# Message passing over 412500 edges: every gather with 125 rows, and one tile in eight groups fetched row by row by SyncE

## The chip, the cores and the metric

The kernel runs on one core of one Trainium2 chip. The metric is the device time of one execution in microseconds. Five engines work side by side, each in the order of its own instructions: TensorE (PE; its weight loads are listed as PEld), VectorE (DVE), ScalarE (ACT), GpSimd (POOL) and SyncE (SP), which here only issues DMAs. They wait for one another by semaphores.

## The reference

One layer of a graph network with 12500 nodes of 64 features and 412500 edges sorted by receiver. For every edge, the features of its sender, its receiver and the edge itself go through two small networks, one for a message and one for a logit; a softmax over all edges weighs the messages, and each receiver sums what it gets.

```python
h = jnp.maximum(_layernorm(x, axis=-1), 0.0)
msg_in = concatenate([h[src], h[dst], edge_attr_32], axis=-1)      # 412500 x 160
messages = swish(msg_in @ W1 + b1) @ W2 + b2
att = softmax(swish(msg_in @ Wa1 + ba1) @ Wa2 + ba2, axis=0)
aggregated = segment_sum(messages * att, dst, num_segments=12500)
out = x + swish(concatenate([h, aggregated], -1) @ Wu1 + bu1) @ Wu2 + bu2
```

## The kernel before

A prologue normalises the nodes and writes two tables to HBM: `ts_d` holds for each node its sender's part of both first layers (128 floats, 512 bytes), `tr_d` the receiver's part. The edges are then cut into 3304 tiles of `EP` = 125, and eight tiles (`K`) make a group `g`; there are 413 groups (`NG`). The loop over the groups is most of the time.

`load(g)` is written two groups ahead of `begin(g)` (`AHEAD`). It issues, on POOL, eight indirect DMAs (line 533) that gather the senders' rows of `ts_d` into `gs`, one of seven buffers of the pool `gather`. Tiles 0, 2, 4, 6 of a group gather 125 rows; tiles 1, 3, 5, 7 gather `WIDE` = 126, the last of which nobody reads. On SyncE it issues two loads of receiver rows into one of three `wins` buffers (line 554), whose address is a register read from `base_sb`, and for every fourth group the edge features (`eo`, line 544) and twice the receivers' numbers (`dbs`, line 547). VectorE turns those into a 0/1 matrix (line 558) and TensorE multiplies it with the window (line 562), which gives `pe`: receiver's part plus edge's part.

`begin(g)` adds the gathered rows to `pe` on VectorE (line 573) and takes the tanh on ScalarE (576). `end(g)` makes messages and logits on VectorE (586 to 597). Some groups later `by_node` builds weights (640) and TensorE sums the messages by receiver into `sp` (646); `out_of` copies `sp` on ScalarE (652), `project` multiplies it with the update's weights (657), and `put` adds the product to a table in SBUF (671, 675). A batch of four groups shares one running maximum of the logits.

All engines' orders are written out (`pin`). A buffer of `gs` is free again when `end` of its group has read it. The set `chosen`, whose tiles would be made from node features in SBUF instead of gathered, is empty in both kernels. Of the DMAs on the hardware queues, eight share eight semaphores in turn: each DMA waits for the one eight places before it, unless that is known to be done. The same holds for POOL's gathers among themselves.

Of the kernel before, what the change touches and what calls it, by code (L numbers as in the profile page):

```python
# [44 lines left out]
F32 = mybir.dt.float32  # L45
I32 = mybir.dt.int32
AF = mybir.ActivationFunctionType
ALU = mybir.AluOpType
AX = mybir.AxisListType
ENG = mybir.EngineType  # L50
# [3 lines left out]
P = 128  # L54
EP = 125
# [3 lines left out]
C = 2 * U  # L59
S1 = U + 1  # L60
K = 8
# [13 lines left out]
PHASE = 1  # L75
SLOTS = (((0, 24), (24, 24)), ((48, 24), (72, 12)), ((84, 24), (108, 17)))
ROUND = 12582912.0
WIDE = 126
EPS = 1e-5
NEG = -3.0e38  # L80
BIG = 3.0e38
# [5 lines left out]
WHY = "a receiver's number; windows past the last node are padded"  # L87
# [3 lines left out]
def gnn_kernel(ctx: ExitStack, tc: tile.TileContext, n_edges, x, src, src_row, dst, dst_row, first, edge,  # L91
# [73 lines left out]
    with tc.tile_pool(name="node1", bufs=1) as node1, \  # L165
# [134 lines left out]
        for c, nn in chunks:  # L300
            tr = node.tile([P, CB, C], F32, name="tr")[:, :nn, :]
            for b in range(0, nn, 4):
                n = min(4, nn - b)
                pn = node_ps.tile([P, 4, C], F32, name="pn", bufs=4)
                for i in range(0, n, 2):
# [7 lines left out]
        pin(nc.scalar.dma_start(hT_d, hT))  # L313

    one_pass(tc, n_edges, locals())
    again = nc.values_load(wrong[0:1, 0:1], min_val=0, max_val=1,
                           skip_runtime_bounds_check_because="it is the outcome of a comparison")
# [76 lines left out]
def one_pass(tc, n_edges, v):  # L394
    nc = tc.nc
    NB, T, NG, NP, NT = (v[k] for k in ("NB", "T", "NG", "NP", "NT"))
    ident, iota_w, bj, dloc, src_full, base_sb, real, unreal, far, wrong = (
        v[k] for k in ("ident", "iota_w", "bj", "dloc", "src_full", "base_sb", "real", "unreal",
                       "far", "wrong"))
    ts_d, tr_d, bq_d, xb_d, edge, dst_row = (  # L400
        v[k] for k in ("ts_d", "tr_d", "bq_d", "xb_d", "edge", "dst_row"))
    wa2, ba2_c, w2b, wu1a, wu2h, we, gather = (
        v[k] for k in ("wa2", "ba2_c", "w2b", "wu1a", "wu2h", "we", "gather"))
# [6 lines left out]
    pin = tc.keep_in_program_order  # L410

    with ExitStack() as ctx:
# [38 lines left out]
        for w in wins:  # L451
            nc.vector.memset(w, 0.0)
            for r in range(2):
                rows = slice(WR + r * DE, WR + (r + 1) * DE)
                nc.vector.tensor_copy(w[rows, :, r, :], we[rows, None, :].to_broadcast([DE, 2, C]))
        with tc.tile_pool(name="work2", bufs=2) as work2, \
                tc.tile_pool(name="small", bufs=3) as small, \
                tc.tile_pool(name="pre_ps", bufs=AHEAD + 1, space=PSUM) as pre_ps, \
                tc.tile_pool(name="one_ps", bufs=1, space=PSUM) as one_ps:
            pes, gss, lgs, ps_, psums, sps, pps, ees, mts, nums, cols = ({} for _ in range(11))  # L460


            w2t_ps = one_ps.tile([P, 4, P], F32, name="mt")[:U, 0, :S1]
# [8 lines left out]
            chosen = set()  # L472
# [23 lines left out]
            def columns(g, first, n):  # L496
                if g not in chosen:
                    return
                to, at = cols[g]
                _, regs = nc.values_load_multi_w_load_instructions(  # L500
                    at[0:1, first:first + n], engines=[ENG.Activation], min_val=0, max_val=NP // 2 - 1,
                    skip_runtime_bounds_check_because=WHY)
                for i in range(n):
                    pin(nc.scalar.copy(to[:, first + i:first + i + 1], hT[:, bass.ds(regs[i], 1)]))

            def burst(g, k):
                for i in range(EVERY):
                    columns(g + 3 + i, *SLOTS[EVERY - 1 - i][k])

            at_sp, at_lo, at_hi, bus, rest = {}, {}, {}, {}, {}  # L510


            tr_w = bass.AP(tensor=tr_d.tensor, offset=tr_d.offset,
                           ap=[[C, NP + WR - SHIFT], [SHIFT * C, 2], [1, C]])

            def registers(g, engine, at, base=base_sb, top=NP - 1):
                n = min(NQ, NG + (base is not base_sb) - g)
                _, regs = nc.values_load_multi_w_load_instructions(
                    base[0:1, g:g + n], engines=[engine], min_val=0, max_val=top,
                    skip_runtime_bounds_check_because=WHY)  # L520
                for i in range(n):
                    at[g + i] = regs[i]

            def load(g):

                t = g * K
                if g % NQ == 0:
                    registers(g, ENG.SP, at_sp)
                full = gather.tile([P, K, C], F32, name="gs")
                gs = gss[g] = full[:EP]  # L530
                for j in range(K - (g in chosen)):
                    rows = WIDE if j % 2 == 1 else EP
                    nc.gpsimd.indirect_dma_start(  # L533
                        out=full[:rows, j, :], out_offset=None, in_=ts_d[:, :],
                        in_offset=bass.IndirectOffsetOnAxis(ap=src_full[:rows, t + j:t + j + 1], axis=0))
                if g % NQ == 0:
                    n = min(NQ, NG - g) * E2
                    eo = eos[g // NQ % 2]
                    i = g // NQ % 2
                    db = dbs[i * WR:(i + 1) * WR].bitcast(I32)  # L540
                    for i in range(g, min(g + NQ, NG)):
                        e = slice((i - g) * E2, (i - g + 1) * E2)
                        ees[i] = eo[:, e], db[:, e]
                    nc.sync.dma_start(eo[WR:, :n],
                                      edge[:, g * E2:g * E2 + n])
                    for r in range(2):
                        nc.sync.dma_start(
                            db[r * R:(r + 1) * R, :n],
                            bass.AP(tensor=dst_row.tensor, offset=dst_row[r:r + 1, g * E2:].offset,
                                    ap=[[0, R], [1, n]]))  # L550
                eo, db = ees.pop(g)
                win = wins[g % WINS]
                for r in range(2):
                    nc.sync.dma_start(win[r * R:(r + 1) * R, :, r, :],
                                      tr_w[bass.ds(at_sp[g], R), :, :])
                for h in range(2):
                    e = slice(h * E2 // 2, (h + 1) * E2 // 2)
                    pin(nc.vector.tensor_scalar(eo[:WR, e], db[:, e], bj[g // NQ % 2 * WR:(g // NQ % 2 + 1) * WR, g, h:h + 1], None,  # L558
                                                op0=ALU.is_equal))
                pe = pes[g] = pre_ps.tile([P, K, C], F32, name="pe")[:EP]  # L560
                for q in range(H):
                    pin(nc.tensor.matmul(pe[:, 2 * q:2 * q + 2, :], eo[:, q * EP:(q + 1) * EP],  # L562
                                         win[:, q // 2, :, :], start=True,
                                         stop=q < H - 1 or g not in chosen))
                if g in chosen:
                    to, _ = cols[g]
                    pin(nc.vector.scalar_tensor_tensor(to, nums[g], half, to, op0=ALU.is_equal, op1=ALU.mult))
                    pin(nc.tensor.matmul(pe[:, K - 1, :], to, stack, start=False, stop=True))

            def begin(g):  # L570

                n = K - (g in chosen)
                pin(nc.vector.tensor_tensor(gss[g][:, :n, :], pes[g][:, :n, :], gss[g][:, :n, :], ALU.add))  # L573
                if n < K:
                    pin(nc.vector.tensor_copy(gss[g][:, n, :], pes[g][:, n, :]))
                pin(nc.scalar.activation(pes[g], gss[g], AF.Tanh))  # L576

            def end(g, then=None):
# [124 lines left out]
            at, weighed = [None, None], [0]  # L703
# [31 lines left out]
            for g in range(AHEAD):  # L735
                load(g)
            done = 0
            for g in range(NG):
# [4 lines left out]
                if more and g == NG - 1:  # L743
                    next(more)
                begin(g)
                if more and g < NG - 1:
                    next(more)
# [9 lines left out]
                if g + AHEAD < NG:  # L757
                    load(g + AHEAD)
# [36 lines left out]
                if g >= 16 and g // 8 - 2 < NT:  # L795
# [3 lines left out]
                    elif g % 8 in (0, 3, 6):  # L799
# [3 lines left out]
                                         engines=[ENG.SP, ENG.DVE, ENG.PE, ENG.Activation])  # L803


            two, one = at[1], at[0]
# [334 lines left out]
```

## Time and profile before

| | before |
|---|---|
| time, three runs | 5157.05, 5168.84, 5172.98 us; median 5168.84 |
| the profiled execution | 5172.98 us; span 5171.3 us, 1.7 us outside it |
| mean granted TensorE clock | 0.595 of full |
| busy: PE, DVE, ACT, POOL | 2470.4, 3165.5, 608.2, 3674.5 us |
| gathers (line 533) | 3304, first at 51.2 us, last at 5068.8 us |
| window loads (line 554) | 826 |
| gather queue, hardware DMA queue | 17.8% and 13.1% of 16 engines' span |

The busy time of an engine counts the instructions themselves. Behind the bar in a group's row stand its busy time and the mean of one in ns, behind the second bar the time that the engine stood idle just before such an instruction, with what ended most of it. "issue" means that the profile shows nothing that the engine waited for, "remote" that a semaphore update ended the wait whose sender the view doesn't name. Beginning and end of the loop take 152.5 us together.

### The profile page before, as it was taken

How to read it: one execution, taken by the hardware profiler on the slowest of the kernel's cores; microseconds unless marked ns; L12 is line 12 of the kernel's file. 1: busy time of each engine (PE TensorE's matmuls, PEld its weight loads, DVE VectorE, ACT ScalarE, POOL GpSimd, SP SyncE). 2: the span in 40 equal slices, each digit the busy share in tenths (PEclk: the TensorE clock that was granted, in tenths of full speed). 3: DMA queues.
4: the chain of work that ended last, by engine and by line, in shares of the span. 5: the costliest groups of instructions: out<-in, count | busy, mean ns of one | idle time of the engine just before them, and what ended most of it. 6: DMA issues, size and time to landing. Idle time of an engine off the chain costs nothing. (4 is left out here: it accounts for less than half of the span.)

```text
span 5171.3 us, 46541 instructions
## 1 busy us (share of the span) xinstructions
PE 2470.4 (48%) x11247; PEld 1946.3 (38%) x11247; DVE 3165.5 (61%) x8745; ACT 608.2 (12%) x1250; POOL 3674.5 (71%) x3329
## 2 busy tenths in 40 slices
PE   5254544544454544444544544444444444444545
PEld 4243433433343433333333433333333333333435
DVE  6366666666665656565655656665656555655757
ACT  3011111111110111111110111111111111110112
POOL 4777677677677677777777777777777777777772
PEclk8555565665555556665655556665656555655656
DMA  7233333333333323323323322322323323323322
GB/s 242 64 80 74 78 88 74 79 80 78 75 74 70 71 64 73 73 67 72 73 66 70 73 67 69 74 67 70 72 65 73 73 64 73 73 65 72 73 66 69
DMA packets 315703, 393.24 MB, mean 76 GB/s; under 512 B 153249, under 2 KB 244478, under 8 KB 315042
## 3 DMA queue, kind: packets, MB, share of 16 engines
q0 software_dynamic: 211456, 214.45, 17.8%
q1 hardware_dynamic: 102594, 166.10, 13.1%
q10 hardware_dynamic: 1376, 9.67, 0.5%
q8 instruction: 92, 1.51, 0.1%
q14 instruction: 185, 1.52, 0.1%
HBM read 362.26 MB, written 25.72 MB: 75 GB/s over the span
## 5 line engine op out<-in xcount | busy, mean ns | idle before, releaser
L533 POOL DMA_INDIRECT gs<-ts_d,src_sb x3304 | 3657.3, 1107 | 1410.1 <-issue 1377.3
L562 PE MATMUL pe<-wins,eo 128*125 128x256 f32 x3304 | 1497.2, 631 | 1055.7 <-issue 453.6
L562 PEld LDWEIGHTS pe<-wins,eo 128*125 128x125 f32 x3304 | 1000.4, 317 | 1348.9 <-issue 518.5
L657 PE MATMUL mt<-ss,w2u 65*128 65x40 f32 x826 | 224.4, 369 | 1336.6 <-issue 703.3
L657 PEld LDWEIGHTS mt<-ss,w2u 65*128 65x128 f32 x826 | 209.4, 293 | 1536.3 <-issue 970.7
L640 DVE TENSOR_SCALAR wt<-iota_w,dloc,p 125x40 f32<-125x40 f32 x3304 | 760.1, 342 | 5.0
L646 PE MATMUL sp<-wt,acts 125*65 125x40 f32 x6608 | 714.6, 286 | 3.6 <-DVE wt L640 2.7
L646 PEld LDWEIGHTS sp<-wt,acts 125*65 125x65 f32 x6608 | 678.9, 205 | 7.7 <-DVE wt L640 3.4
L675 DVE TENSOR_TENSOR sums<-sums,mt 64x40 f32 x606 | 116.0, 191 | 854.1 <-remote 734.0
L576 ACT ACTIVATE pe<-gs 125x1024 f32<-125x1024 f32 x413 | 424.7, 1028 | 1600.3 <-DVE gs L573 759.1
L573 DVE TENSOR_TENSOR gs<-pe,gs 125x1024 f32<-125x1024 f32 x413 | 503.1, 1218 | 50.3 <-issue 30.7
L671 DVE SCALAR_TENSOR_TENSOR sums<-sums,scale,mt 64x40 f32 x220 | 56.1, 255 | 594.5 <-remote 446.3
L652 ACT COPY ss<-sp 65x40 f32<-65x40 f32 x413 | 77.4, 187 | 2543.9 <-remote 2380.3
L592 DVE SCALAR_TENSOR_TENSOR pe<-pe,gs 125x512 f32<-125x512 f32 x413 | 288.9, 699 | 14.0
L594 DVE TENSOR_TENSOR pe<-pe,w_all 125x512 f32<-125x512 f32 x413 | 288.7, 699 | 13.8
L586 DVE SCALAR_TENSOR_TENSOR acts<-pe,gs 125x512 f32<-125x512 f32 x413 | 285.6, 692 | 15.7 <-issue 3.1
L597 DVE TENSOR_REDUCE lg<-pe 125x8 f32<-125x512 f32 x413 | 284.0, 688 | 11.0
L558 DVE TENSOR_SCALAR eo<-dbs,bj 64x250 f32<-64x250 int32 x826 | 274.4, 372 | 16.1 <-DMA dbs<-in_dst_row_dram 7.8
L678 DVE COPY stand<-nmax 64x40 f32 x826 | 181.8, 220 | 2.0 <-issue 1.4
L616 PE MATMUL mt<-ident,mx 125*128 125x125 f32 x110 | 46.4, 421 | 269.7 <-remote 124.5
L623 DVE TENSOR_REDUCE gm<-mt 128x1 f32<-128x125 f32 x110 | 31.1, 282 | 200.7 <-remote 200.1
L357 DVE TENSOR_SCALAR bu<-mt,w_all 64x256 f32<-64x256 f32 (+1 forms) x50 | 23.9, 478 | 170.0 <-remote 124.6
(113 smaller groups left out, 571.3 us busy)
## 6 DMA issues: line engine op xcount, KB each, us to landing
gs<-ts_d,src_sb POOLq DMA_INDIRECT x3304
eo<-in_edge_dram SPq DMA_DIRECT2D x103, 500.0 KB
dbs<-in_dst_row_dram SPq DMA_DIRECT2D x206, 250.0 KB
wins<-tr_d SPq DMA_DIRECT2D x826, 32.0 KB
ts_d<-ts SPq DMA_DIRECT2D x5, 896.0 KB
tr_d<-tr ACTq DMA_DIRECT2D x5, 896.0 KB
hT_d<-hT ACTq DMA_DIRECT2D x1, 3136.0 KB
xt<-in_x_dram SPq DMA_DIRECT2D x24, 128.0 KB
```

The source lines that it names most:

```text
L533: nc.gpsimd.indirect_dma_start(out=full[:rows, j, :], out_offset=None, in_=ts_d[:, :], in_offset=bass.IndirectOffsetOnAxis(ap=src_full[:ro ...
L558: pin(nc.vector.tensor_scalar(eo[:WR, e], db[:, e], bj[g // NQ % 2 * WR:(g // NQ % 2 + 1) * WR, g, h:h + 1], None, op0=ALU.is_equal))
L562: pin(nc.tensor.matmul(pe[:, 2 * q:2 * q + 2, :], eo[:, q * EP:(q + 1) * EP], win[:, q // 2, :, :], start=True, stop=q < H - 1 or g not in ...
L573: pin(nc.vector.tensor_tensor(gss[g][:, :n, :], pes[g][:, :n, :], gss[g][:, :n, :], ALU.add))
L576: pin(nc.scalar.activation(pes[g], gss[g], AF.Tanh))
L586: pin(nc.vector.scalar_tensor_tensor(acts[g % ACTS][:, :, 0:U], th[:, :, U:C], 1.0, gs[:, :, U:C], op0=ALU.add, op1=ALU.mult))
L592: pin(nc.vector.scalar_tensor_tensor(att, th[:, :, 0:U], 1.0, gs[:, :, 0:U], op0=ALU.add, op1=ALU.mult))
L594: pin(nc.vector.tensor_tensor(att, att, wa2[:EP, None, :].to_broadcast([EP, K, U]), ALU.mult))
L597: pin(nc.vector.tensor_reduce(lgs[s][:, k:k + K], att, AX.X, ALU.add))
L640: pin(nc.vector.tensor_scalar(wt[:, j, :], iota_w[:EP, j // H, :], dloc[:, g * K + j:g * K + j + 1], p[:, k + j:k + j + 1], op0=ALU.is_equ ...
L646: pin(nc.tensor.matmul(sp, acts[g % ACTS][:, j, :], wt[:, j, :], start=j == 0, stop=j == K - 1))
L657: pin(nc.tensor.matmul(pp, w2u.rearrange("s h u -> s (h u)"), sps.pop(g), start=True, stop=True))
```

## The change

All gathers have 125 rows. In groups 8, 16, ..., 408 (51 of them) the last tile is not gathered by POOL: SyncE fetches its 125 rows one at a time into a buffer of its own, `alone[g]`. The eight groups before it share that work: in each `load`, behind the window loads, SyncE reads up to 16 row numbers into registers (line 540) and issues as many DMAs of one row, 512 bytes (line 546). The row numbers of a tile come by one small DMA some groups earlier. `begin(g)` of such a group adds seven tiles at once and the eighth by an addition of its own.

```diff
-WIDE = 126
+QUEUES = [(ENG.SP, 8, 0, 16)]
...
+            def single(q, g):
+                if g < NG - 4:
+                    t = g * K + K - 1 - (g in chosen)
+                    rows_at[q, g] = small.tile([1, EP], I32, name=f"one_src{q}", bufs=2)
+                    nc.sync.dma_start(rows_at[q, g], v["src_row"][:, t * EP:(t + 1) * EP])
+
+            def rows(q, g):
+                engine, every, phase, n_rows = QUEUES[q]
+                if g == 0:
+                    single(q, phase + every)
+                if g < phase:
+                    return
+                at = (g - phase) % every
+                g = g - at + every
+                if at == 0:
+                    rows_at.pop((q, g - every), None)
+                    if (q, g) in rows_at:
+                        alone[g] = work2.tile([EP, C], F32, name=f"one_gs{q}")
+                if at == every // 2:
+                    single(q, g + every)
+                if (q, g) not in rows_at:
+                    return
+                a = at * n_rows
+                n = min(n_rows, EP - a)
+                if n <= 0:
+                    return
+                loads, regs = nc.values_load_multi_w_load_instructions(
+                    rows_at[q, g][0:1, a:a + n], engines=[engine], min_val=0, max_val=NP - 1,
+                    skip_runtime_bounds_check_because=WHY)
+                for one in loads:
+                    pin(one)
+                for k in range(n):
+                    pin(dma[engine].dma_start(alone[g][a + k:a + k + 1, :], ts_d[bass.ds(regs[k], 1), :]))
...
-                full = gather.tile([P, K, C], F32, name="gs")
-                gs = gss[g] = full[:EP]
-                for j in range(K - (g in chosen)):
-                    rows = WIDE if j % 2 == 1 else EP
+                gs = gss[g] = gather.tile([P, K, C], F32, name="gs")[:EP]
+                for j in range(K - (g in chosen) - (g in alone)):
                     nc.gpsimd.indirect_dma_start(
-                        out=full[:rows, j, :], out_offset=None, in_=ts_d[:, :],
-                        in_offset=bass.IndirectOffsetOnAxis(ap=src_full[:rows, t + j:t + j + 1], axis=0))
+                        out=gs[:, j, :], out_offset=None, in_=ts_d[:, :],
+                        in_offset=bass.IndirectOffsetOnAxis(ap=src_sb[:, t + j:t + j + 1], axis=0))
...
                 for r in range(2):
                     nc.sync.dma_start(win[r * R:(r + 1) * R, :, r, :],
                                       tr_w[bass.ds(at_sp[g], R), :, :])
+                for q in range(len(QUEUES)):
+                    if QUEUES[q][0] == ENG.SP:
+                        rows(q, g)
...
             def begin(g):
-                n = K - (g in chosen)
+                n = K - (g in chosen) - (g in alone)
                 pin(nc.vector.tensor_tensor(gss[g][:, :n, :], pes[g][:, :n, :], gss[g][:, :n, :], ALU.add))
+                if g in alone:
+                    pin(nc.vector.tensor_tensor(gss[g][:, n, :], pes[g][:, n, :], alone.pop(g), ALU.add))
```

More of the change, by code (lines that the diff above doesn't have):

```diff
@@ L396, in one_pass @@
     NB, T, NG, NP, NT = (v[k] for k in ("NB", "T", "NG", "NP", "NT"))
-    ident, iota_w, bj, dloc, src_full, base_sb, real, unreal, far, wrong = (
-        v[k] for k in ("ident", "iota_w", "bj", "dloc", "src_full", "base_sb", "real", "unreal",
+    ident, iota_w, bj, dloc, src_sb, base_sb, real, unreal, far, wrong = (
+        v[k] for k in ("ident", "iota_w", "bj", "dloc", "src_sb", "base_sb", "real", "unreal",
                        "far", "wrong"))
@@ L459, in one_pass @@
                 tc.tile_pool(name="one_ps", bufs=1, space=PSUM) as one_ps:
-            pes, gss, lgs, ps_, psums, sps, pps, ees, mts, nums, cols = ({} for _ in range(11))
+            pes, gss, lgs, ps_, psums, sps, pps, ees, mts, nums, cols, alone = ({} for _ in range(12))
             w2t_ps = one_ps.tile([P, 4, P], F32, name="mt")[:U, 0, :S1]
@@ L508, in burst @@
                     columns(g + 3 + i, *SLOTS[EVERY - 1 - i][k])
+            rows_at = {}
+            dma = {ENG.SP: nc.sync, ENG.Activation: nc.scalar}
+            def single(q, g):
[30 more added lines that the diff above has]
+                    pin(dma[engine].dma_start(alone[g][a + k:a + k + 1, :], ts_d[bass.ds(regs[k], 1), :]))
             at_sp, at_lo, at_hi, bus, rest = {}, {}, {}, {}, {}
@@ L570, in begin @@
             def begin(g):
-                n = K - (g in chosen)
+                n = K - (g in chosen) - (g in alone)
                 pin(nc.vector.tensor_tensor(gss[g][:, :n, :], pes[g][:, :n, :], gss[g][:, :n, :], ALU.add))
-                if n < K:
-                    pin(nc.vector.tensor_copy(gss[g][:, n, :], pes[g][:, n, :]))
+                if g in alone:
+                    pin(nc.vector.tensor_tensor(gss[g][:, n, :], pes[g][:, n, :], alone.pop(g), ALU.add))
+                if g in chosen:
+                    pin(nc.vector.tensor_copy(gss[g][:, K - 1, :], pes[g][:, K - 1, :]))
                 pin(nc.scalar.activation(pes[g], gss[g], AF.Tanh))
```

## The prediction

> **What bounds the kernel now.** I read the page's table of engines first, then its costliest groups, then the waits, then the timeline of one cycle.
>
> ```profile
> span 5171.3 us, 46541 instructions
> ...
> PE 2470.4 (48%) x11247; PEld 1946.3 (38%) x11247; DVE 3165.5 (61%) x8745; ACT 608.2 (12%) x1250; POOL 3674.5 (71%) x3329
> ...
> L533 POOL DMA_INDIRECT gs<-ts_d,src_sb x3304 | 3657.3, 1107 | 1410.1 <-issue 1377.3
> ```
>
> POOL does one thing, the 3304 gathers, and looks 71% busy. Its idle time says more: 1410 us are mostly the 0.30 us that follow each gather (3303 x 0.30 = 1000 us). Another 49 us lie before the first gather, and 359 us remain (85 gaps in the trace): there POOL stands before a group's first gather because none of the seven `gs` buffers is free. So neither side is the bound alone. POOL would need 11.3 us a group, the loop takes 12.15 us (5018.8 us from first gather to last, over 413 groups), and POOL is held up now and then by the consumers.
>
> ```profile
> ACT ss L652 <- remote: 2380.3, 246, 27.0
> POOL gs L533 <- issue: 1377.3, 3246, 48.8
> ```
>
> The consumers are held up too, by something that this view can't name ("remote"). The timeline shows it at the end of one cycle (start, us, then the instruction and the idle time before it):
>
> ```profile
> 2616.24 1.21 DVE L573 TENSOR_TENSOR gs<-pe,gs 125x1024 f32<-125x1024 f32 x1
> ...
> 2622.42 1.96 PE L646 MATMUL sp<-wt,acts 125*65 125x40 f32 x16
> ...
> 2640.25 1.21 POOL L533 DMA_INDIRECT gs<-ts_d,src_sb  x1 [0.30 <-issue]
> 2641.76 1.00 POOL L533 DMA_INDIRECT gs<-ts_d,src_sb  x1 [0.30 <-issue]
> 2644.58 0.19 ACT L652 COPY ss<-sp 65x40 f32<-65x40 f32 x1 [21.48 <-remote]
> ...
> 2646.28 1.21 DVE L573 TENSOR_TENSOR gs<-pe,gs 125x1024 f32<-125x1024 f32 x1
> ...
> 2652.57 1.21 POOL L533 DMA_INDIRECT gs<-ts_d,src_sb  x1 [9.81 <-issue]
> 2653.81 1.23 DVE L573 TENSOR_TENSOR gs<-pe,gs 125x1024 f32<-125x1024 f32 x1 [0.19 <-issue]
> ```
>
> The matmuls into `sp` were put through at 2622.4. ScalarE's copy of `sp` starts 22 us later, two microseconds after POOL has stopped. Between, the semaphore updates recorded for TensorE come about one per gather: of 3155 gaps between them in the run, 734 are 1.3 to 1.6 us. When POOL stops, the rest arrives at once. The group that began (L573) at 2616.24 therefore waits 30 us for its successor, while the next takes 7.5 us. One cycle of eight groups, between the stalls that end at 2552.61 and 2652.57, has four groups of 7.2 to 7.8 us and four of 17.4 us on average: 100 us, of which POOL's 64 gathers are 90 and a stall 9.8.
>
> **First part: 125 rows for 126.** The timeline gives the price of one row. The durations alternate, and the even tile of a pair is the 125-row one:
>
> ```profile
> 2637.43 1.21 POOL L533 DMA_INDIRECT gs<-ts_d,src_sb  x1 [0.30 <-issue]
> 2638.94 1.00 POOL L533 DMA_INDIRECT gs<-ts_d,src_sb  x1 [0.30 <-issue]
> ```
>
> Start to start, in the 3218 spacings without a stall, a 125-row gather takes 1.518 us and a 126-row gather 1.304: the wider one is 0.214 us cheaper. Each group loses four cheap ones; of the 1652, 51 disappear in the second part, so 1601 x 0.214 = **+342 us** of POOL time.
>
> The Trainium skill, page "DMA: Bandwidth & Descriptors", section "Why a DMA increments its semaphore by 16 and not by 1", says that a DMA is spread over the largest number of engines up to 16 that divides its rows: 5 for 125, 14 for 126. The packets of this trace agree: 47908 of 4096 B and 31388 of 512 B on the gather queue, 14.5 and 9.5 a gather, the means of 5 x (3 + 1) and 14 x (1 + 1) packets. The page prices no gather; were the price one per data packet, 125 rows (20 packets) would be cheaper than 126 (28), this term would be at most nothing, and the sum would end at 5106.
>
> **Second part: one tile in eight groups leaves POOL.** Groups 8, 16, ..., 408 gather seven tiles. That is 51 gathers fewer, always the eighth, a 126-row one: 51 x 1.304 = **-67 us**. POOL then needs 3253 x 1.518 / 413 = 11.96 us a group.
>
> **What SyncE takes over.** Each of those tiles costs 125 one-row DMAs, each with its register instruction, 16 a group behind the group's two window loads, one load of 16 registers a group, and one load of row numbers per eight groups. The nearest row is the second window load, which is also addressed by a register:
>
> ```profile
> L554 SPq MOVE wins<-tr_d x826: 3/29/1345, 81.3 to 5078.4; - x166
> L554 SPq DMA_DIRECT2D wins<-tr_d x826: 4/317/1685, 81.3 to 5078.5; - x166
> ```
>
> From the start of the first to the start of the second it is 0.52 us where POOL is idle (57 pairs), 0.74 on average while POOL gathers (356 pairs), median of all 0.65. A DMA of a single row in the prologue (`base_sb`) took 0.31 us to issue, like the 0.32 here, so a smaller transfer will not be cheaper. SyncE's group holds 15.6 rows, two windows, 0.9 of the other loads (rounded into 18.5 DMAs) and some 0.3 us of register loads: 9.9 us at 0.52, 12.3 at 0.65, 14.0 at 0.74. The loop after the change takes (5018.8 + 275) / 413 = 12.8 us a group. It is covered by SyncE's idle time (it mostly waits for TensorE to free a window) as long as a DMA costs under (12.8 - 0.3) / 18.5 = 0.68 us. I take 0.65, the median, and so nothing on the path; if the cover is gone, see the first rival. Every row DMA also waits for the DMA eight before it. A window's last packet starts 1.2 us after issue, and eight issues take 4 us, so that wait is met, except behind the edge load (4.2 us, once in four groups). Behind a waiting row stand the next group's window loads, for which TensorE waits; three window buffers give them about two groups of slack.
>
> The page named above also says, under "Rules for kernel authors", to coalesce small transfers, and gives a fixed cost of some 2.0 us per DMA. Taken one after another, that would be an estimated 250 us a tile, or 31 us a group, and a time above 12000. The trace issues the next DMA after 0.5 to 0.7 us.
>
> **VectorE** gets 51 extra additions of 125x128 (0.2 to 0.35 us by its small rows) and the first addition shrinks by an eighth of 1.22 us in the same groups: within 10 us either way, covered by its 39% idle time.
>
> **POOL's stalls.** The sum turns on the 359 us. Both ends: all gone (-359), if the consumers stay at 12.15 us a group; grown, if SyncE joins them. I keep them, because in the slow half of a cycle the consumers are clocked by the gathers: about one TensorE update per gather. A gather that takes 1.518 instead of 1.411 us makes the four slow groups 7.6% longer: 69.6 x 0.076 = 5.3 us per 100, or 5019 x 0.053 = +266 us. That is the same as the POOL sum, 342 - 67 = +275, reached from the other side.
>
> **Sum:** own time of the profiled run 5173.0 (span 5171.3 and 1.7 outside), plus 275 = **5448 us**. The median shown is 5168.8, 4 us lower, within the spread of the runs.
>
> **The rivals.** *SyncE becomes the bound (slower still).* It decides from 0.68 us a DMA. For it: the mean with POOL busy is 0.74, and its slow cases look clocked by the gathers as well. Against: the median is under the limit, and a loop that lags gives POOL pauses in which a DMA costs 0.52. At 0.74 a group fits 16.2 DMAs into POOL's 11.96 us and the other 2.3 at 0.52 into a pause: 13.5 us with the register loads, 413 x 13.46 + 152.5 outside the loop + 1.7 = 5713. *The stalls are eaten up (faster).* If the slow half is not clocked by gathers but by a fixed time, the consumers keep 12.15 us, POOL's 11.96 fills their time, and both terms pass without stalls: 5173 + 275 - 359 = 5089. It turns faster from the point where over 275 of the 359 us are absorbed. For it: POOL's own need stays below the consumers' present pace. Against: the recorded updates keep step with the gathers. *The width is not what makes the odd gather cheap.* If it is the place in a pair, the mean of 1.411 stays, and 51 x 1.411 = -72 us gives 5101. Against: nothing else differs between the two, and the packets do.
>
> **How the numbers follow.** Stalls kept: 0.50, 5448. Half of them absorbed: 0.05, 5270. SyncE the bound: 0.26, 5570 to 5720. Absorbed: 0.14, 5089. Width without effect: 0.05, 5101. A measurement of this kernel can tell about 0.3%, 15 us, from no change; a landing there needs stalls absorbed almost exactly, 0.03 taken from the two faster cases. So faster 0.16, same 0.03, slower 0.81. The range goes from 5140 to 5720: it leaves out the two faster cases and a little above the dearest SyncE.
>
> **What would show it.** Right: all gathers 1.21 us and none of 1.00, 3253 of them, POOL near 3960 us busy, stalls of about 360 us still there, L652's wait not shorter. Wrong: mean gather under 1.15 us; stalls gone; or POOL's stalls above 500 us with TensorE waiting for `wins`, which would be SyncE.

## The result and the profile after

The changed kernel takes 5052.34 us (5051.23 to 5052.72, four runs), the kernel before in the same comparison 5167.32 us (5157.05 to 5172.98): a ratio of 0.978, 95% interval 0.976 to 0.980. The forecast was 5448 us, slower.

One thing must be known to read these numbers. The kernel before takes about 5160 us in the recorded pair and on chip 13, and 4762 to 4771 us on chips 0, 3, 4, 14 and 15. The one profile of it from there (chip 3) has under 4 us of pauses in which POOL stands before a full set of buffers. Against that faster before, the changed kernel is 5.8% slower (below).

The page of after, its engines and the groups that answer to those of before:

```profile
span 5050.3 us, 66258 instructions
...
PE 2353.8 (47%) x11247; PEld 1896.7 (38%) x11247; DVE 3219.3 (64%) x8796; ACT 589.2 (12%) x1250; POOL 3964.8 (79%) x3278
...
L569 POOL DMA_INDIRECT gs<-ts_d,src_sb x3253 | 3947.6, 1214 | 1044.1 <-issue 947.7
```

The gathers (now line 569) are as forecast: 3253 of them, POOL 3965 us busy, 1.21 us each. But idle before them is 1044 us, and 3252 gaps of 0.305 us are 992 of it. The first wait for the table is another 48. Only 4 us are left of the 359 that POOL stood before a group. The waits and the timeline say the same (start, us, instruction, and in brackets the idle time before it):

```profile
DVE gs L612 <- DMA gs<-ts_d,src_sb: 1449.4, 350, 7.5
POOL gs L569 <- issue: 947.7, 3104, 0.3
```

```profile
2614.85 1.21 POOL L569 DMA_INDIRECT gs<-ts_d,src_sb  x1 [0.30 <-issue]
2616.37 1.21 POOL L569 DMA_INDIRECT gs<-ts_d,src_sb  x1 [0.30 <-issue]
2617.03 1.22 DVE L612 TENSOR_TENSOR gs<-pe,gs 125x1024 f32<-125x1024 f32 x1 [3.50 <-DMA gs<-ts_d,src_sb]
2617.89 1.21 POOL L569 DMA_INDIRECT gs<-ts_d,src_sb  x1 [0.31 <-issue]
2619.26 0.18 ACT L693 COPY ss<-sp 65x40 f32<-65x40 f32 x1
```

The direction of waiting has turned. VectorE waits for gathers in 350 of the 413 groups, the longest pause between two gathers is 2.4 us where it was 12.6, and the copy of `sp`, which had waited 2380 us for "remote" updates, starts without a bracket. (The 48.8 us in before's "issue" row is the wait for the table ahead of the first gather; after's row books that wait under the table's DMA.) POOL's gathers alone set the time. In the spans: gathers without their pauses +276 us (3253 x 1.518 for 1652 x 1.518 + 1652 x 1.304), pauses 359 to 4, -355, and the stretch behind the last gather's start 102 to 57 us, because the consumers no longer trail the gathers (the addition to `pe` began 52 to 67 us behind its group's last gather in most groups, now 2 to 7), -45. The sum is -124, measured 5050.3 - 5171.3 = -121.

### The profile page after: what moved, and what is told of

Its sections match the earlier page's. It is cut to its first block, busy times and chain, and to the rows that moved or that the text cites. A ratio compares the mean times of both kernels' runs of the same rounds, so it can differ in the third digit from the quotient of the medians.

```text
span 5050.3 us, 66258 instructions
## 1 busy us (share of the span) xinstructions
PE 2353.8 (47%) x11247; PEld 1896.7 (38%) x11247; DVE 3219.3 (64%) x8796; ACT 589.2 (12%) x1250; POOL 3964.8 (79%) x3278
## 5 line engine op out<-in xcount | busy, mean ns | idle before, releaser
L569 POOL DMA_INDIRECT gs<-ts_d,src_sb x3253 | 3947.6, 1214 | 1044.1 <-issue 947.7
L601 PE MATMUL pe<-wins,eo 128*125 128x256 f32 x3304 | 1527.3, 641 | 1746.5 <-DVE eo L597 1091.6
L601 PEld LDWEIGHTS pe<-wins,eo 128*125 128x125 f32 x3304 | 1022.2, 325 | 2049.0 <-DVE eo L597 1188.3
L612 DVE TENSOR_TENSOR gs<-pe,gs 125x1024 f32<-125x1024 f32 (+1 forms) x413 | 498.7, 1208 | 1463.1 <-DMA gs<-ts_d,src_sb 1449.4
L687 PE MATMUL sp<-wt,acts 125*65 125x40 f32 x6608 | 628.7, 266 | 8.8 <-DVE wt L681 4.9
L687 PEld LDWEIGHTS sp<-wt,acts 125*65 125x65 f32 x6608 | 591.2, 181 | 16.3 <-DVE wt L681 7.1
L597 DVE TENSOR_SCALAR eo<-dbs,bj 64x250 f32<-64x250 int32 x826 | 296.1, 398 | 85.2 <-DMA dbs<-in_dst_row_dram 77.7
L698 PE MATMUL mt<-ss,w2u 65*128 65x40 f32 x826 | 186.0, 319 | 197.9 <-DVE gm L664 160.7
L719 DVE COPY stand<-nmax 64x40 f32 x826 | 212.7, 257 | 0.8 <-issue 0.2
L668 ACT ACTIVATE scale<-fall 128x1 f32<-128x1 f32 x110 | 22.4, 204 | 581.2 <-DVE nmax L665 274.0
```

Source lines behind the costliest of these rows:

```text
L569: nc.gpsimd.indirect_dma_start(out=gs[:, j, :], out_offset=None, in_=ts_d[:, :], in_offset=bass.IndirectOffsetOnAxis(ap=src_sb[:, t + j:t ...
L687: pin(nc.tensor.matmul(sp, acts[g % ACTS][:, j, :], wt[:, j, :], start=j == 0, stop=j == K - 1))
L698: pin(nc.tensor.matmul(pp, w2u.rearrange("s h u -> s (h u)"), sps.pop(g), start=True, stop=True))
```

## The experiments

Two questions: do the two gather terms hold, and what removed the pauses? All kernels are the changed one with the width of each of a group's eight gathers, `WIDTHS`, and the list `QUEUES` set as said; with `QUEUES` empty SyncE fetches no rows and POOL gathers 3304 tiles. `before` and `after` were also run unchanged. Where an expected text names a theory by a letter, what is compared here is the time that it gives. "Hold-up" is the lateness of TensorE's semaphore updates that the forecast saw in before's trace. In e5 the seven buffers are also named one by one and cleared at the start, because ten of their rows are never gathered.

**Each part alone, and other widths** (chip 4, before 4763.28 us).

```diff
-QUEUES = [(ENG.SP, 8, 0, 16)]
+QUEUES = []
+WIDTHS = (125,) * 8               # e1
+WIDTHS = (126,) * 8               # e3
+WIDTHS = (115,) * 8               # e5: ten rows of each tile are not gathered
+                                  # e2: QUEUES kept, WIDTHS = (125, 126) * 4
```

> The first part alone: every tile gathered with 125 rows, no tile by SyncE. Theory A (the 14-engine gathers of 126 rows are what holds up TensorE's semaphore updates): the hold-up is gone as in the changed kernel, POOL is busy without a pause, and the 51 gathers that come back cost 51 x 1.518 = 77 us more than the changed kernel: 5050 + 77 = 5129 us; ScalarE's wait before the copy of sp stays near 60 us in all. Theory B (SyncE's row DMAs are what removed the hold-up): the waits before the copy of sp come back with over 1500 us, POOL pauses for 300 us or more, 5450 to 5520 us. Theory C (POOL's faster pace caused it: 11.3 us a group against 11.96): at 12.14 us a group it is gone too, 5129 us.

Measured 5115.84 us, ratio 1.074 (1.072 to 1.076). Over before +352.6 us; 1652 x 0.214 is 353.5.

> The second part alone: one tile in eight groups by SyncE, and the odd tiles still gather 126 rows. Theory A: the hold-up stays (over 1500 us of waiting before the copy of sp, POOL pauses of 300 us or more), and the time stays within some 100 us of the kernel before: 5070 to 5250 us. Theory B: no hold-up, POOL's own pace is the time: 1652 x 1.518 + 1601 x 1.304 + 110 outside = 4705 us. Theory C: POOL is even quicker than before (11.13 us a group), so the hold-up stays, 5070 to 5250 us.

Measured 4695.9 us, ratio 0.986 (0.984 to 0.987): -67.4 us, and 51 x 1.304 is 66.5.

> Every tile gathered with 126 rows, no tile by SyncE: twice as many wide gathers as before. POOL alone would need 3304 x 1.304 + 110 = 4418 us. Theory A: the hold-up is at least as long as before, 5150 us or more, and the gain in POOL's pace turns into pauses of POOL (600 us or more). Theory C: the same sign, as POOL is faster still. If both are wrong and the hold-up comes from the alternation of the two widths, it is gone and the time is 4420 to 4600 us.

Measured 4409.39 us, ratio 0.926 (0.924 to 0.927).

> Every tile gathers only its first 115 rows (115 is divided by 5 and by nothing more up to 16, like 125); the last ten rows of each tile are left at zero or stale, so ten edges of each tile are computed without their sender. A gather should take about 1.0 to 1.15 us and 0.30 us behind it, so that POOL's pace is about the 1.41 us of the kernel before, without wide gathers. Theory A (number of engines): no hold-up, POOL busy without a pause, 3304 x 1.36 to 1.43 + 110 = 4600 to 4850 us. Theory C (pace): at the pace of before the hold-up returns, over 1500 us of waiting before the copy of sp, and 5100 us or more.

Measured 5025.59 us, ratio 1.055 (1.053 to 1.057). The gather rows of e3 and e5:

```profile
L572 POOL DMA_INDIRECT gs<-ts_d,src_sb x3304 | 3291.6, 996 | 1056.4 <-issue 963.6
```

```profile
L581 POOL DMA_INDIRECT gs<-ts_d,src_sb x3304 | 3905.5, 1182 | 1061.0 <-issue 899.3
```

126 rows cost 0.996 us and 115 rows 1.182: fewer rows, dearer gather. In all four the idle time before gathers is, to 3 us, only their 0.30 us each and the first wait, and the times follow POOL's sum. Both terms of the forecast hold, each to 1 us. The expectations of 5150 or more for e3 fall: wide gathers do not make POOL pause on this chip, and neither does the mix of before, which ran beside them at 4763.

**The pair again, and 128 and 127 rows** (chip 3, before 4761.94 us over 13 runs).

```diff
+WIDTHS = (128,) * 8               # f1, QUEUES kept
+WIDTHS = (127,) * 8               # f3, QUEUES = []
```

> The kernel before, unchanged, for a profile beside the one shown. Theory D (the hold-up of TensorE's updates is a state that the alternating gathers can be in or not, independent of the kernel's text): either the profile shows the hold-up and 5157 to 5173 us again, or none of it and POOL's own pace as the time: 1652 x 1.518 + 1652 x 1.304 + 110 = 4772 us. Theory E (the hold-up always comes with this kernel): ScalarE's wait before the copy of sp near 2400 us and over 5100 us whatever the chip.

Measured 4762.46 us, ratio 1.000 (0.999 to 1.001). Its waits beside the recorded ones of before show what is missing:

```profile
DVE gs L573 <- DMA gs<-ts_d,src_sb: 1288.9, 369, 8.7
...
POOL gs L533 <- issue: 947.4, 2953, 47.8
```

Same instructions, same gathers (1.104 us on average, recorded 1.107), but no "remote" wait at all, and VectorE waits for gathers. Of TensorE's recorded updates, 32 gaps are 1.3 to 1.6 us, where the recorded profile has 734. So the kernel alone does not bring the hold-up.

> The changed kernel, unchanged, on the same chip as the repeated kernel before. If POOL's gathers alone set the time, it is 3253 x 1.518 + 112 = 5050 us whatever the state of the kernel before; against a kernel before without the hold-up that is 1.060 of its time (slower), against one with it 0.978 (faster).

Measured 5039.7 us, ratio 1.058 (1.057 to 1.060): +277.8 us over before, where the forecast's two gather terms gave +275.

> Every tile gathered with 128 rows (three of them read by nobody), and one tile in eight groups by SyncE as in the changed kernel. If a gather's price follows the rows that one DMA engine gets (25 for 125 rows: 1.210 us; 23 for 115: 1.182; 9 for 126: 0.996; a line of 0.876 + 0.0134 a row), 128 rows over 16 engines give 8 and 0.983 us: 3253 x (0.983 + 0.304) + 112 = 4299 us, faster than both kernels. If 126 is special and 128 is not cheaper, 4350 us or more.

Measured 4267.01 us, ratio 0.896 (0.895 to 0.898).

> Every tile gathered with 127 rows, a prime, no tile by SyncE. If the price follows the rows per engine, one engine gets all 127: 0.876 + 0.0134 x 127 = 2.58 us a gather, 3304 x 2.88 + 110 = 9640 us. If it follows the number of rows, a gather stays near 1.0 to 1.2 us and the time under 5200 us. No theory of the hold-up is at stake here: at such a pace POOL is the bound in all of them.

One run: 9537.19 us. Gather rows of f1 and f3:

```profile
L572 POOL DMA_INDIRECT gs<-ts_d,src_sb x3253 | 3080.1, 947 | 1078.4 <-issue 952.1
```

```profile
L572 POOL DMA_INDIRECT gs<-ts_d,src_sb x3304 | 8418.8, 2548 | 1057.4 <-issue 1001.9
```

127 rows cost 2.55 us, 128 rows 0.95. That fits the rule that the forecast quoted from the Trainium skill ("DMA: Bandwidth & Descriptors", "Why a DMA increments its semaphore by 16 and not by 1"), the largest divisor up to 16: rows per engine are then 127, 25, 23, 9 and 8 for 127, 125, 115, 126 and 128 rows, and 0.876 us + 0.0134 us for each of them gives 2.58, 1.21, 1.18, 1.00 and 0.98 us, measured 2.55, 1.21, 1.18, 1.00 and 0.95. The line was drawn through 125, 115 and 126 rows, and 127 and 128 then tested it. The packets in the five traces show the spread itself: a gather of 127 rows moves its data in 15 packets of 4096 B and one of 3584, which is 127 rows of 512 B on one engine; 128 rows are 16 packets of 4096 B, eight rows on each of 16. The traces also have packets of 4 to 32 B. In a gather of 127 rows they hold, beside 16 of 4 B, 15 times 127 times 4 B, as if each of the other 15 engines got a small entry for every row of the busy one. Whether it is these entries that POOL's time goes by was not tested.

**A chip with the hold-up** (chip 13, before 5157.5 us over 7 runs, 5140 to 5178).

```diff
+WIDTHS = (128,) * 8               # f2, QUEUES = []
+                if g == 40:       # g1: the kernel before, and in begin(40), ahead of its tanh
...
+                    for _ in range(120):
+                        pin(nc.scalar.activation(slow, zeros[:, 0:1].to_broadcast([P, 512]), AF.Copy))
```

> All eight gathers of a group take 128 rows (three of them rows that nothing reads), and no row is fetched by SyncE. Theory 'price by rows per DMA engine, nothing held up': 3304 x (0.947 + 0.304) = 4133 plus some 107 around, 4240 us, so a little under the 4267 of the same kernel with 51 gathers replaced by SyncE's rows, since there TensorE waited 641 us in all for wins, which SyncE issues late. Rival 'POOL bounds still': replacing 51 gathers saves 51 x 1.25 = 64 us with 128 rows too, so this one gives about 4330.

Measured 5708.74 us, ratio 1.105 (1.101 to 1.110): both expectations are off by over 1300 us, because this chip holds updates up. The page's gather row, two waits and a stretch of the timeline:

```profile
L572 POOL DMA_INDIRECT gs<-ts_d,src_sb x3304 | 3126.8, 946 | 2482.9 <-issue 2458.5
```

```profile
ACT ss L696 <- remote: 2560.7, 165, 23.7
POOL gs L572 <- issue: 2458.5, 3224, 48.0
```

```profile
2589.14 1.43 PE L690 MATMUL sp<-wt,acts 125*65 125x40 f32 x16
...
2611.39 0.94 POOL L572 DMA_INDIRECT gs<-ts_d,src_sb  x1 [0.30 <-issue]
2616.62 0.19 ACT L696 COPY ss<-sp 65x40 f32<-65x40 f32 x1 [22.89 <-remote]
2617.03 0.62 PE L701 MATMUL mt<-ss,w2u 65*128 65x40 f32 x2 [19.87 <-DVE gm L667]
...
2623.84 0.94 POOL L572 DMA_INDIRECT gs<-ts_d,src_sb  x1 [11.50 <-issue]
```

The picture is before's, much larger: the matmuls into `sp` were through at 2590.6, and the copy of `sp` starts 26 us later, after POOL's last gather; POOL itself stands 11.5 us until a buffer is free. In the trace's records, 1854 of TensorE's 3125 updates lie in the 151 pauses of POOL longer than 3 us (1452 us in all, 1.28 per us), against 0.30 per us in the rest. In the recorded profile of before it is 1.69 per us in such pauses and 0.54 elsewhere. So on a chip that holds updates up, they come mostly while POOL is not gathering. That the stop lets them through is likely and not shown: POOL stands until a buffer is free, and for that updates must have come. Nor does a slower TensorE explain the late copies: in before's recorded profile the granted clock was 0.595 and a window matmul took 0.631 us on average, on chip 3 0.618 and 0.639.

> The kernel before with 120 more ScalarE copies of 128x512 at group 40, whose results nothing reads: they put the consumers once some 50 to 70 us behind the gathers, as they are all through the recorded profile of before. Theory 'lag feeds itself' (a consumer that is behind stays clocked by the gathers): POOL pauses for buffers to the end, over 4900 us, with updates of TensorE 1.3 to 1.6 us apart. Rival 'the state is set from outside the program': the lag is worked off within some tens of groups, 4762 plus at most 60 us.

Measured 5220.21 us, ratio 1.011 (1.006 to 1.016): inconclusive, since before has its pauses on this chip without the added lag.

**Separating width, pace and SyncE's rows.** These were meant for a chip with the hold-up, but all of them ran on chips without it (before 4762.35 to 4770.64 us).

```diff
+WIDTHS = (128,) * 8               # h1, h1c, QUEUES = []; behind each gather:
+                    pin(nc.gpsimd.memset(idle[:, :160], 0.0))
```

> All gathers of 125 rows, no row by SyncE: the change without its second part. If the kernel before stands at 5157 to 5173 here too (TensorE's updates late), theory 'late updates go with the gathers' spread over the DMA engines' (5 engines for 125 rows, 14 for 126, 16 for 128): the narrower gathers alone take POOL's pauses away, 3304 x 1.518 + 107 = 5122 us, 45 under before. Rival 'SyncE's rows take them away': the pauses stay, over 5300. If before stands at 4763, 5116 as before.

Measured 5114.2 us on chip 14, ratio 1.074 (1.072 to 1.076). The same kernel with the same question took 5116.95 us on chip 4 (e1c), 5120.88 on chip 15 (e1d) and 5113.26 on chip 0 (e1e); before stood at 4762 to 4771 beside each, so the question was not answered.

> 125 and 126 rows in turn as before, with 51 gathers given to SyncE's rows: the change's second part alone, for a chip on which before stands at 5157 to 5173. Theory 'spread': POOL still pauses for buffers, so the gathers saved are given back as pauses, 5100 to 5200 us. Rival 'SyncE's rows take the pauses away': 4700 us. (Where before stands at 4763 it is 4696, as measured.)

Measured 4695.81 us, ratio 0.986 (0.983 to 0.989), as e2.

> All gathers of 128 rows, no row by SyncE, and behind each gather a POOL fill of 128x160 whose result nothing reads, so that gathers follow each other in about 1.5 us, as those of 125 rows do. Where before stands at 5157 to 5173: theory 'spread over 16 engines holds TensorE's updates up whatever the pace' keeps POOL pausing for buffers, 5500 us or more (5709 without the fill); rival 'pace' (gathers that come less often leave the updates room) has no pauses, 3304 x 1.52 + 107, some 5120 or less. Where before stands at 4763: paced by POOL, 5000 to 5130 by both.

Measured 4641.17 us, ratio 0.974 (0.973 to 0.976). The fill took 0.25 us, but the gap behind it shrank to 0.17, so gathers followed each other in 1.37 us and not 1.5, and 3304 x 1.3715 plus 109 outside is 4640.

> All gathers of 128 rows with a POOL fill of 128x160 behind each, 1.37 us apart, for a chip on which before stands at 5157 to 5173 and 128 rows without the fill at 5709. Theory 'spread over 16 engines holds TensorE's updates up whatever the pace': 5500 us or more. Rival 'what counts is the share of time in which POOL starts no gather': the fill leaves 0.42 us in 1.37 free in place of 0.30 in 1.25, so the pauses shrink, 4700 to 5000 us. (Where before stands at 4763 it is 4641, as measured.)

Measured 4639.32 us, ratio 0.974 (0.971 to 0.977): the same on chip 4, where it could not answer its question either.

> All gathers of 128 rows, no row by SyncE, once more: 5709 us on chip 13, where before takes 5157. Theory 'the chip sets whether TensorE's updates come late, and then the widest spread suffers most': where before stands at 4763 nothing is late, 3304 x (0.947 + 0.304) + 107 = 4240 us. Rival 'POOL outruns its consumers with gathers this cheap on any chip': 4500 or more, with POOL pausing for buffers.

Measured 4239.34 us on chip 15, ratio 0.889 (0.886 to 0.892), within 1 us of the first theory. Its gather row against f2's:

```profile
L572 POOL DMA_INDIRECT gs<-ts_d,src_sb x3304 | 3119.9, 944 | 1055.8 <-issue 940.7
```

One kernel, 5709 us on one chip and 4239 on another, with gathers of the same length: the 1427 us of pauses are not the kernel's work. Where nothing is held up this version is the fastest of the study; where it is, it is 551 us slower than before. With SyncE's rows (f1, on chip 3) it takes 28 us more, though 51 gathers fewer should save 64. There TensorE waits 641 us for `wins`, which SyncE issues among its rows (23 us in f2b), the consumers trail POOL by some 44 us, POOL pauses for 39 us, and the stretch behind the last gather's start is 99 us, not 57. With gathers this cheap, the rows no longer pay.

## Why the prediction was wrong

**The gather terms were right.** +342 and -67 us, measured alone as +352.6 (all 1652 tiles) and -67.4, and together as +277.8 against +275 (a2 and its before). The rival without effect of width (5101) falls with e1 and e3.

**The failed step is "POOL's stalls: I keep them".** It took the lateness of TensorE's updates for something paced by the gathers, one update per gather, and let it grow with them. It shrank instead: the pauses it was to keep went from 359 to 4 us, and with the 45 us at the end that accounts for the miss of 396 us. The traces tell how late an update is at least, by the time from the end of the last TensorE instruction that makes one. Over 0.2 us late are 2068 of the 3156 updates recorded in before (66%) and 285 of 2402 in after (12%); in every trace from chips 0, 3, 4, 14 and 15, of any width or pace, it is 2 of about 3500. So the recorded changed kernel did run where updates are held up, but the lateness no longer reaches the buffers. These counts, and those of gaps above, are of incomplete records: the kernel makes about 3620 such updates, and in the traces with the hold-up 39 to 50% of VectorE's are missing too. Those of VectorE and ScalarE that are there come on time (over 0.2 us late: 2 of 3276 and 1 of 563 in before). The mechanism of the rival "the stalls are eaten up" (0.14, 5089 us) is what came: POOL's own need of 11.96 us a group is what the loop takes (4943 us from first gather to last, over 413). Its reason was that the consumers keep 12.15 us; they did better, with updates that came sooner. The rival missed the 45 us at the end, which come from the same cause, since consumers that keep up have less to finish behind the last gather.

**Second failing: one profile was taken for the kernel.** The step that read 359 us of pauses as belonging to before could not have been checked in that profile alone. Without them its sum would have been 4763 + 275 = 5038, and the measurement there is 5039.7.

**SyncE was priced too dear, without harm.** A row DMA was put at 0.65 us and 0.68 was the limit. The recorded trace of after has a median of 0.41 us from one row DMA's start to the next, but the load of 16 registers, put at 0.3, took 1.16 us. By the forecast's own sum that is 18.5 x 0.41 + 1.16 = 8.7 us a group instead of 12.3 (10.3 with the mean of 0.49 within a group). The DMA waits it adds are small:

```profile
PE pe L601 <- DMA wins<-tr_d: 185.4, 35, 11.7
...
PE pe L601 <- DMA one_gs<-ts_d: 57.6, 8, 23.6
```

POOL hides them. The rival "SyncE becomes the bound" (0.26) falls. **VectorE's** 51 additions stayed covered.

**What stays open.** Why some chips let TensorE's updates through late is not known, nor on which chip the recorded pair ran. On such chips pauses were 4 us with 125 rows, 359 with 125 and 126 in turn (404 in g1) and 1427 with 128. (The changed kernel counts as run on such a chip by its late updates.) That order fits the spread of a gather over DMA engines (5, 5 and 14, 16) as well as its pace (one in 1.52, 1.41, 1.25 us), and SyncE's rows were only in the first. Which of the three keeps the pauses away was not shown.

## What to carry to other kernels

Count the rows that an indirect gather leaves on each DMA engine before counting its rows: padding 125 to 128 made each gather 0.26 us cheaper, and the kernel 17% shorter where POOL set the time (e1d 5121 to f2b 4239 us, both on chip 15). But where updates come late the cheaper gather brought pauses: 128 rows took 551 us more than before on chip 13. A wait whose releaser the profile can't name, and whose end follows another engine's pause, may be the chip's and not the kernel's: time the kernel before on a second chip before a stall is kept, or removed, in a sum.

## What the hardware showed unexpectedly

The time of an indirect gather on POOL did not follow its number of rows: 2.55 us for 127, 1.21 for 125, 1.18 for 115, 1.00 for 126, 0.95 for 128. And semaphore updates of TensorE came some 20 to 26 us late on chip 13 and in the recorded before while POOL gathered, and on five other chips not; the same 128-row kernel took 5709 and 4239 us.
